# Three tiles move beside layer 0's buffers, and ScalarE writes the ones columns

## The chip, the core and the metric

The kernel runs on one core of one Trainium2 chip. The core has a matrix engine (TensorE, "PE" in the profile; its weight loads are "PEld"), a vector engine (VectorE, "DVE"), a scalar engine (ScalarE, "ACT"), a general engine (GpSimd, "POOL") and a sync engine (SyncE, "SP") that here only issues transfers. Each engine takes its instructions in a fixed order, and semaphores order the engines among each other. Transfers between device memory and the on-chip buffer (SBUF) are issued from SP ("SPq") or from ScalarE ("ACTq"). TensorE writes to PSUM, a second small memory, from which VectorE and ScalarE read. The metric is the time of one execution on the device in microseconds (us).

## The reference, cut to what matters

There are 16 graphs (batches) of 1024 nodes with 128 features each (`x`), and a symmetric 0/1 matrix `adj` per graph. Four layers follow one another, each as `x = layernorm(x + layer(x, adj))`:

```
layer 0:  w = row softmax of adj^T where adj^T != 0
          region = batchnorm((w @ x) @ K1 + b1);  people = batchnorm((w^T @ region) @ K2 + b2)
layer 1:  h = x W + b;  e = leaky_relu(h a1 + (h a2)^T + b_a) where adj > 0
          softmax over axis 1;  relu(attention @ h)
layers 2, 3:  scores = leaky_relu((h * a_k) @ h^T) where adj == k+1 (k = 0..3)
          softmax over the last axis;  alpha @ h
```

The two batch norms of layer 0 take their mean and variance over all 16 graphs and all nodes. So layer 0 has to pass over all graphs before its second norm is known, and only then can any graph go on to its residual, its layer norm and layers 1 to 3.

## The kernel before

`fast_path` (from L554) serves inputs whose matrix holds only zeros and ones; a check at its end calls `general_path` otherwise, and that isn't executed here.

**Layer 0 (L646 to L788).** Two pools of buffers, `f_l0` and `f_l0c`, are open. For each batch the kernel loads the matrix and its transpose (`load_adj`, L722, tiles `f_at` and `f_att` of 1 MB each, six buffers each) from SP, multiplies them on TensorE with three bf16 parts of the features (`product`, L733), sums the parts on VectorE (L736), and accumulates Gram matrices on TensorE (`gram`, L665). The result of each batch, `f_yf`, is written to a scratch array in device memory, `f_people`, from ScalarE's queue (L775).

**Between the layers (L790 to L835).** From the Gram matrix (copied out by ScalarE, L669) and a few sums a short chain computes the second batch norm: TensorE L800 to L808, VectorE L811 to L816, L602 and L603, then an inverse square root on GpSimd (`rsqrt`, L596 and L597), VectorE L606 to L609, three small products on TensorE (`on_rows`, L826). It ends in `f_m` (L829), the matrix that the batch's `people` values are to be multiplied with, and in two tiles of rows, `f_shift2_rows` (L831) and `f_row_rows` (L834).

**Layers 1 to 3 (from L840).** The pools of layer 0 are closed by then, and a pool `f_lanes` is opened over the same bytes. It holds three lanes (`Lane`, L843), so that three batches are under way at once, and tiles that all lanes share. A first access to a tile of that pool has to wait until everything that used the closed pools is done, the last write of `f_people` among it. The tiles that matter here are:

- `rows` (two per lane, L851): 1024 rows of 129 columns; the last column holds ones (written by GpSimd, L853), so that the products of layers 2 and 3 (L1206) give the sum of the weights along with the result;
- `xt` (one per lane, L854): turned rows, 128 x 1024;
- `nothing` (L872): zeros for an empty product (L1085);
- `yn` and `x0` (L876, one buffer each, shared by all batches): a batch's `people` values, read back from device memory (L1007), and its original features (L1009).

The profile leaves trailing numbers of tile names out: `x0` is `f_x` in its lines, `xt` is `f_xt`.

For each batch the steps after layer 0 begin with two loads (`yn`, then `x0`, on SP). VectorE adds the shift and the bias to `x0` (L1011, then eight times L1014). In three groups of rows TensorE turns `yn` (L980), ScalarE copies the turned rows to `xt` (L993), TensorE multiplies them with `f_m` (L1023), VectorE adds `x0` and writes `rows` (L1031). A layer norm follows (L906, L908, L918 to L924), the normed rows are turned in their turn (L980, L993), and layer 1 starts (L1056).

**Order.** All steps from there on are given to `Plan` (L107), which takes written starting times (`BEGIN`, `WHEN`) and costs, works out one order per engine, and ties each engine's instructions to that order. Layer 0 and the work between the layers aren't under it. They, and the plan's instructions among them, are put in order by the framework's own scheduler, which starts what is ready and prefers what stands earlier in the program. The profile shows such a move: VectorE executes L1238, from the very end of the program, at 395.04 us. The classes of shared tiles, their numbers and the plan's data stay as they are in this change.

## Time and profile before

| what | us |
|---|---|
| median of three runs | 1717.28 (1714.45 to 1718.93) |
| the profiled execution's own time | 1720.13 |
| its span, first to last instruction | 1718.2 |
| layer 0 and the work between the layers | from 0 to about 431 |
| last `f_people` write, issue (L775) | 423.57 |
| first load of `yn`, issue (L1007) | 427.24 |
| first load of `x0`, issue (L1009) | 427.64 |
| first product with `f_m` (L1023) | 432.38 |
| first product of layer 1 (L1056) | 446.81 |

The time outside the span is 1720.13 - 1718.2 = 1.9 us. TensorE is busy for 94% of the span, VectorE for 77%, ScalarE for 62%, GpSimd for 20%. The page's second part cuts the span into 40 slices of 43 us, and slice 10, from 430 us on, is the one in which TensorE is least busy (5 tenths, at 6 tenths of its clock): that is where layer 0 hands over to the lanes.

In a line of the timeline the first column is the start in us, the second the length in us (of the whole group where a line stands for several instructions, "xN"), then the engine, the line of the kernel, the operation and the tiles "out<-in". A bracket gives the idle time of the engine before it and what ended that.

### The profile page before, as it was taken

To read this page: it belongs to the slowest core of one execution; us is meant where nothing else is said; L and a number is where in the kernel's file an instruction comes from. 1 tells how busy PE (TensorE), PEld (TensorE's weight loads), DVE (VectorE), ACT (ScalarE), POOL (GpSimd) and SP (SyncE) were. 2 spreads that over 40 slices of the span, in tenths; PEclk is the share of its full clock that TensorE was granted. 3 is DMA by queue.
4 is the path that set the end of the run, shared out by engine and by line. 5 is a ranking of instruction groups with operands and counts; after the bars stand their busy time and mean duration, and the time that the engine had idled before them with its cause. 6 is when DMAs were issued, how large, how long until landed. Compare 5 with 4: busy or idle time off the path is not lost. (4 is left out here: it accounts for less than half of the span.)

```text
span 1718.2 us, 34517 instructions
## 1 busy us (share of the span) xinstructions
PE 1618.3 (94%) x13007; PEld 1450.2 (84%) x13023; DVE 1325.3 (77%) x2940; ACT 1070.8 (62%) x2697; POOL 339.3 (20%) x621
## 2 busy tenths in 40 slices
PE   6999999999569999999999999999999999999996
PEld 4666666666459999999999999999999999999995
DVE  4565575565558889898988989898898989888764
ACT  6555545642235767767676776767667676767664
POOL 0000000000222131323223232332314132231310
PEclk9999999999679999999999999999999999999998
DMA  8999999996355657677666767776676777666651
GB/s 306 381 370 390 361 377 381 368 384 224 132 167 173 200 172 219 196 208 212 208 196 187 219 194 212 209 210 191 190 216 195 205 215 211 189 180 202 183 161 52
DMA packets 394641, 397.14 MB, mean 231 GB/s; under 512 B 10592, under 2 KB 339168, under 8 KB 394464
## 3 DMA queue, kind: packets, MB, share of 16 engines
q1 hardware_dynamic: 377824, 386.45, 69.3%
q10 hardware_dynamic: 16640, 8.39, 1.6%
q8 instruction: 104, 1.70, 0.4%
q14 instruction: 73, 0.60, 0.1%
HBM read 377.89 MB, written 16.91 MB: 230 GB/s over the span
## 5 line engine op out<-in xcount | busy, mean ns | idle before, releaser
L1206 PE MATMUL f_pbank<-f_rows,f_p 128*128 128x129 f32 x4096 | 497.2, 274 | 1.7 <-ACT f_xt L993 1.0
L1206 PEld LDWEIGHTS f_pbank<-f_rows,f_p 128*128 128x128 f32 x4096 | 476.6, 191 | 2.9 <-ACT f_xt L993 1.4
L1156 PE MATMUL f_pbig<-f_xt,f_hw 128*128 128x128 f32 x2304 | 305.2, 277 | 3.5 <-ACT f_hw L995 2.5
L1156 PEld LDWEIGHTS f_pbig<-f_xt,f_hw 128*128 128x128 f32 x2304 | 282.5, 193 | 4.8 <-ACT f_hw L995 3.0
L1106 PE MATMUL f_pbig<-f_q,f_p 128*128 128x128 f32 x2048 | 258.8, 281 | 18.4 <-ACT f_q L1100 18.3
L1185 DVE TENSOR_TENSOR f_q<-f_q,f_e 128x1024 f32<-128x1024 f32 (+7 forms) x256 | 193.5, 756 | 103.7 <-ACT f_q L1178 67.0
L1178 ACT ACTIVATE f_q<-f_pbig,f_neg_shift 128x1024 f32<-128x1024 f32 (+7 forms) x256 | 189.0, 738 | 127.9 <-PE f_pbig L1170 123.2
L1106 PEld LDWEIGHTS f_pbig<-f_q,f_p 128*128 128x128 f32 x2048 | 246.7, 197 | 20.8 <-ACT f_q L1100 20.4
L1182 ACT ACTIVATE f_e<-f_pbig,f_neg_shift 128x1024 f32<-128x1024 f32 (+7 forms) x256 | 188.5, 736 | 58.5 <-PE f_pbig L1170 53.6
L1193 DVE TENSOR_TENSOR f_p<-f_q,f_a 128x1024 f32<-128x1024 f32 (+7 forms) x256 | 192.3, 751 | 2.1 <-issue 0.2
L733 PE MATMUL f_pz<-f_xs,f_at 128*128 128x390 bf16 x1024 | 180.5, 332 | 4.8 <-DVE f_xs L716 4.2
L733 PE MATMUL f_pz<-f_zs,f_att 128*128 128x390 bf16 x1024 | 181.0, 328 | 3.1 <-DVE f_yf L736 2.9
L754 ACT ACTIVATE f_junk<-f_at,f_sq_bias 128x1024 bf16<-128x1024 int32 x128 | 146.9, 1148 | 51.8 <-DVE f_yf L736 48.4
L1091 DVE SCALAR_TENSOR_TENSOR f_p<-f_u,f_r,f_u 128x1024 f32<-128x1024 f32 x128 | 162.8, 1272 | 2.1 <-DMA f_u<-f_u_dram 2.0
L733 PEld LDWEIGHTS <-f_at 128*128 128x128 fp8e4 x1024 | 100.6, 98 | 73.9 <-issue 7.8
L733 PEld LDWEIGHTS <-f_att 128*128 128x128 fp8e4 x1024 | 100.0, 98 | 69.6 <-issue 6.5
L1094 DVE SCALAR_TENSOR_TENSOR f_p<-f_p,f_a 128x1024 f32<-128x1024 f32 x128 | 155.8, 1217 | 0.8
L1197 DVE TENSOR_TENSOR f_p<-f_pbig,f_a 128x128 f32<-128x128 f32 (+6 forms) x224 | 152.1, 679 | 0.0
L736 DVE TENSOR_REDUCE f_zr<-f_pz 128x129 f32<-128x387 f32 x128 | 63.2, 551 | 113.3 <-PE f_pz L733 113.2
L1170 PE MATMUL f_pbig<-f_ident,f_q 128*128 128x128 f32 x896 | 135.5, 273 | 4.2 <-DVE f_q L1185 3.3
L968 POOL TENSOR_SCALAR f_ln_var<-f_sq 128x3 f32<-128x3 f32 (+2 forms) x96 | 35.6, 371 | 505.2 <-ACT f_junk L957 505.2
L993 ACT COPY f_xt<-f_pbank 128x512 f32<-128x512 f32 (+2 forms) x192 | 83.2, 441 | 71.8 <-PE f_pbank L980 71.7
(165 smaller groups left out, 2079.2 us busy)
## 6 DMA issues: line engine op xcount, KB each, us to landing
f_a<-in_adjt_dram SPq DMA_DIRECT2D x384, 512.0 KB, 4.7
f_at<-in_adj_dram SPq DMA_DIRECT2D x64, 1024.0 KB, 9.1
f_att<-in_adjt_dram SPq DMA_DIRECT2D x64, 1024.0 KB, 13.6
f_u<-f_u_dram SPq DMA_DIRECT2D x32, 512.0 KB, 6.2
f_xn<-in_x_dram SPq DMA_DIRECT2D x16, 512.0 KB, 11.2
f_people<-f_yf ACTq DMA_DIRECT2D x16, 512.0 KB, 16.9
f_yn<-f_people SPq DMA_DIRECT2D x16, 512.0 KB, 3.8
f_x<-in_x_dram SPq DMA_DIRECT2D x16, 512.0 KB, 6.6
```

Source lines behind the costliest of these rows:

```text
L733: nc.tensor.matmul(pz[:, :3 * K], a8[:, j % 2, c * 512:(c + 1) * 512:4], moving[:, j].rearrange("p k d -> p (k d)"), start=(j == 0), stop= ...
L754: nc.scalar.activation(junk, at[c // 2][:, c % 2, :], AF.Square, bias=sq_bias, accum_out=squares[:, b, c:c + 1])
L1091: p = op(DVE, 1.2, lambda e, t, t2, *_, j=j: nc.vector.scalar_tensor_tensor(e, t2, ln.r[:, j:j + 1], t, ALU.mult, ALU.max), [key("r", j)], ...
L1094: op(DVE, 1.24, lambda t, e, j=j: nc.vector.scalar_tensor_tensor(e, e, 1.0, t.rearrange("p c n -> p (c n)"), ALU.mult, ALU.mult, accum_out ...
L1106: nc.tensor.matmul(t[:, c * D:(c + 1) * D], q[:, c * P:(c + 1) * P], hn[:, j, :], start=False, stop=(j == C - 1 and c % 4 == 3))
L1156: nc.tensor.matmul(t[:, j * P:(j + 1) * P], hw[:, j * P:(j + 1) * P], xt[:, mine], start=True, stop=True)
L1178: nc.scalar.activation(q[:, blocks, :], t[:, c * P:].rearrange("p (c n) -> p c n", n=P), AF.Exp, bias=neg_shift)
L1182: nc.scalar.activation(e[:, c * P:], t[:, c * P:], AF.Exp, bias=neg_shift, scale=SLOPE)
L1185: nc.vector.tensor_max(q[:, blocks, :], q[:, blocks, :], e[:, c * P:].rearrange("p (c n) -> p c n", n=P))
L1193: nc.vector.tensor_mul(t[:, c * P:].rearrange("p (c n) -> p c n", n=P), q[:, blocks, :], k[:, c:, :])
L1197: nc.vector.tensor_mul(t[:, :c * P].rearrange("p (c n) -> p c n", n=P), s[:, :c * P].rearrange("p (c n) -> p c n", n=P), k[:, :c, :])
L1206: nc.tensor.matmul(t[:, :D + 1], w[:, j * P:(j + 1) * P], xl[:, j, :], start=(j == 0), stop=(j == C - 1))
```

## The change

Four edits, all in `fast_path`:

1. `nothing` and its zeroing by GpSimd move from after the lanes to the constants at the start of the function.
2. Three tiles, `yn`, `x0` and `xt0` (4 KB per partition each), are taken from the pool of constants, which is open all along, so their bytes aren't shared with layer 0's buffers. `yn` and `x0` are the shared tiles of before under the same names; `xt0` becomes the `xt` of lane 0. The other two lanes keep theirs in the pool of lanes. All later tiles move by 13 KB per partition.
3. The six columns of ones are written by ScalarE, as a copy of eight columns of a tile of ones, in place of six GpSimd memsets.
4. The classes `yn` and `x0` of the plan are given the new tiles.

```diff
 LANES = 3
+EARLY = ("yn", "x0", "xt0")
...
+    nothing = const.tile([P, 512], BF16, name="f_nothing")
+    nc.gpsimd.memset(nothing, 0.0)
+
+    early = {name: const.tile([P, C, D], F32, name=f"f_{name}") for name in EARLY}
+
     sums = const.tile([P, 3, B * C], F32, name="f_sums")
...
             for t in self.rows:
-                nc.gpsimd.memset(t[:, :, D:D + 1], 1.0)
-            self.xt = tile([P, N], "xt")
+                nc.scalar.copy(t[:, :, D], ones[:, :C])
+            self.xt = early["xt0"].rearrange("p c n -> p (c n)") if i == 0 else tile([P, N], "xt")
...
-    nothing = lanes.tile([P, 512], BF16, name="f_nothing")
-    nc.gpsimd.memset(nothing, 0.0)
...
-    for cls, n in (("yn", 1), ("x0", 1)):
-        plan.tiles(cls, [lanes.tile([P, C, D], F32, name=f"f_{cls}{i}") for i in range(n)])
+    for cls in ("yn", "x0"):
+        plan.tiles(cls, [early[cls]])
```

## The prediction

> **What bounds the kernel now.** I read the page's first two parts, then busy times by stretch, then the timeline and the waits around 430 us, where layer 0 hands over to the lanes.

> ```profile
> span 1718.2 us, 34517 instructions
> PE   6999999999569999999999999999999999999996
> PEclk9999999999679999999999999999999999999998
> DMA  8999999996355657677666767776676777666651
> ```

> TensorE bounds both long stages, at 9 tenths or more in nearly every slice. The dip in slices 10 and 11 is the handover, where the time goes by a chain of waits and not by any engine's work. Busy time by stretch (start and end, length, then busy us of PE, PEld, DVE, ACT and POOL with instruction counts, the granted clock, DMA share, GB/s):

> ```profile
> 423.50:427.20 3.70, 2.73 (x23) 2.44 (x22) 1.55 (x9) 0.27 (x1) 0.19 (x1) 0.97 0.49 142
> 427.20:450.80 23.60, 14.32 (x54) 11.49 (x54) 9.91 (x41) 7.16 (x20) 5.65 (x21) 0.50 0.29 90
> 450.80:515.00 64.20, 35.92 (x206) 32.56 (x209) 39.06 (x93) 19.96 (x67) 18.12 (x24) 0.77 0.50 169
> ```

> From 427.20 to 450.80 no engine is busy for more than 14.32 of 23.60 us, and the clock is at half. The change acts there. Its timeline:

> ```profile
> 407.09 0.88 SPq L722 DMA_DIRECT2D f_att<-in_adjt_dram  x2
> ...
> 423.57 0.52 ACTq L775 DMA_DIRECT2D f_people<-f_yf  x1
> ...
> 427.24 0.34 SPq L1007 DMA_DIRECT2D f_yn<-f_people  x1
> 427.35 0.29 POOL L853 MEMSET f_rows<- 128x8 f32 x6 [3.55 <-DMA f_people<-f_yf]
> 427.46 0.16 DVE L603 TENSOR_TENSOR f_bn_var<-f_got,f_bn_var 128x1 f32<-128x1 f32 x1
> 427.56 0.52 POOL L873 MEMSET f_nothing<- 128x512 bf16 x1
> 427.64 0.43 SPq L1009 DMA_DIRECT2D f_x<-in_x_dram  x1
> 428.05 0.19 POOL L596 TENSOR_SCALAR f_rs_t<-f_bn_var 128x1 f32<-128x1 f32 x1
> ...
> 430.31 0.29 DVE L829 TENSOR_TENSOR f_m<-f_m,f_pacc 128x128 f32<-128x128 f32 x1 [0.42 <-PE f_pacc L826]
> 430.79 0.27 ACT L831 COPY f_shift_rows<-f_pacc 128x128 f32<-128x128 f32 x1 [5.76 <-PE f_pacc L826]
> ...
> 430.92 0.85 PE L980 MATMUL f_pbank<-f_ident,f_yn 128*128 128x128 f32 x3
> ...
> 431.85 0.48 ACT L993 COPY f_xt<-f_pbank 128x384 f32<-128x384 f32 x1 [0.42 <-PE f_pbank L980]
> ...
> 432.38 1.65 PE L1023 MATMUL f_pbank<-f_m,f_xt 128*128 128x128 f32 x6 [0.61 <-ACT f_xt L993]
> 433.01 1.23 DVE L1011 TENSOR_TENSOR f_x<-f_x,f_shift_rows 128x1024 f32<-128x1024 f32 x1 [2.41 <-DMA f_x<-in_x_dram]
> ...
> 437.74 0.69 DVE L1031 TENSOR_TENSOR f_rows<-f_pbank,f_x 128x512 f32<-128x512 f32 x1 [0.74 <-PE f_pbank L1023]
> ```

> See three things. The `yn` load, the first memset and everything else that touches the lanes' pool start at about 427.2, when the last `f_people` write has landed. GpSimd's inverse square root, on the path to `f_m`, starts when the memsets end, though its input was there at 427.46 + 0.16 = 427.62. And between `f_m` (430.31 + 0.29 = 430.60) and the first product with it (432.38) stand the turns of `yn` and the copy to `xt`, while VectorE waits for `x0` until 433.01.

> **The change part by part**

> *The two loads.* Outside the shared bytes, `x0` waits for nothing and `yn` for batch 0's write of `f_people`, issued at 56.0. SP takes instructions in order; the scheduler prefers what stands earlier in the program, and all layer 0 loads do. I therefore place both behind the last `f_att` issue, at 407.09 + 0.88 = 408.0. SP has nothing to do then until 427.24, so nothing is queued behind them that is late; the third load of the plan, the second `yn`, still waits for L980. Landing now takes about 3.8 us for a `yn` and 5.2 us for this `x0`; behind the `f_att` loads and beside the 408.70 `f_people` write (whose kind takes 3.5 to 17.8 us) I bound it by 17.8: on chip by 426, before anybody asks. Cost there: nothing, covered by 15 us in which TensorE multiplies tiles whose loads are ahead in the same queue. At worst the 1 MB delays that `f_people` write, which nobody waits for.

> [...]

> *The inverse square root.* Six memsets (0.29 us together) and `f_nothing` (0.52) leave GpSimd's queue there. The hop from L603 to L596 in the first norm was 0.1 us (415.02 to 415.11), so L596 starts at 427.71 instead of 428.05: 0.34 us gained for `f_m`, `f_shift2_rows` and `f_row_rows`. The zeroing of `nothing` at the start costs GpSimd 0.52 us beside loads whose first product comes at 14.8: nothing.

> *The ones on ScalarE.* Six copies of 128x8. The nearest rows are L1064 (170 ns for 128x3) and L1075 (255 ns for 16x128): 1.0 to 1.5 us. They wait for the landing at 427.2 and so end by 428.8. ScalarE is idle from 425.03 to 430.79 (the 5.76 us in L831's bracket), now to 430.45: hidden, with 1.6 us to spare. Behind them stand L993 or L831; if that cover were gone they would cost at most 1.5 us.

> *The turned rows.* `xt0` is free and `yn` is there, so the first group's turns need only a PSUM bank, which layer 0 gives up with ScalarE's copy L669 (424.76 + 0.27 = 425.03). TensorE is idle from about 426.6 to 429.5. Three turns (0.85 us at half clock, less at full) and the copy (0.48) fit in there. Should the turns stand ahead of L808 they delay the norm by up to 0.3 us (three at the full-clock pace of 0.11 us); I take 0. The plan's order lets only this one group go ahead: the second group's turns stand behind the first product with `f_m`.

> *The sum on the path.* TensorE's `on_rows` products end their issue 0.34 earlier; the last of six starts at 430.70 and one follows each 0.21 us, so L1023 starts at 430.70 - 0.34 + 0.21 = 430.57, `f_m` being ready at 430.26. It started at 432.38: 1.81 us gained. L1011 starts behind L831, at 430.79 + 0.27 - 0.34 + 0.08 = 430.80 and not at 433.01: 2.2 us gained, so `x0` isn't late any more. Next late is TensorE: L1031 of the second group waited 0.74 us for L1023 already, and its turns and products follow L1023 at an unchanged pace. The gain is the smaller, 1.81 us. Everything behind (the norm, layer 1's start at 446.81, the second `yn` load at 437.88, the loads of `u`) follows by waits on this chain, in an unchanged order, so I carry 1.8 us to the end.

> Against the profiled execution: 1720.1 - 1.8 = 1718.3 us. That execution stands 2.85 us over the median of the runs (1717.28), so the time is 1717.3 - 1.8 = 1715.5, with 1.5 (turns ahead of L808) and 2.2 (TensorE gains with `x0`) as its ends.

> **The rivals**

> *The clock comes back earlier.* It is at half for 23.9 us from 427.0 on and changes several more times until 515.7, always at ends of stretches of about 3.4 us. Work between 427.2 and 450.8 keeps TensorE busy for 14.32 us; one more such stretch at full clock saves at most 1.7 us, and in the ramp to 515 (clock 0.77) a second one as much. For it: the chain's products stand closer together. Against it: the idle gaps behind 436 stay. Time: 1717.3 - 1.8 - 1.7 to 3.4 = 1712.1 to 1713.8, take 1713. A row can't tell where the 3.4 us stretches will lie in another run; the same slip can cost 1.7.

> [...]

> *The loads are not freed.* If the scratch array counts as one whole, `yn` still waits for the last `f_people` write and lands at 430.7, `x0` behind it at 432.9. Then only the 0.34 us remain: 1717.0. Against it: nothing in the layer 0 rows ties one batch's write to the next's.

> *The loads stand among layer 0's (the other side).* If the scheduler puts `yn` in an earlier gap of SP, SP stands still there until the `f_people` write has landed, 16.9 us in the median, while layer 0 is short of room: DMA is at 9 tenths or more, and TensorE has no wait on loads there. Once the block and 1 MB more (2.8 us at the 370 GB/s of those slices) exceed the lead of the loads over the products, TensorE stops. Price between 0 and 16.9 + 2.8 = 19.7; the nearest row is SP's present wait on `f_people`, 15.4 us per batch, which TensorE survives without a wait, so most is covered: I take 5 us. Time: 1717.3 - 1.8 + 5 = 1720.5. It decides from a stop of 1.8 us on. Against it: full queues leave SP no gap in which a later load would be preferred.

> *The ones stand ahead of L669 on ScalarE.* L669 (424.76) would then wait for 427.2 and six copies: 427.2 + 1.5 - 424.8 = 3.9 us later, and all behind it: 1719.4. Against it: GpSimd's memsets are executed behind later work of layer 0, and L669 is ready first.

> **How the numbers follow.** Chances: 1.8 us gained 0.58, clock 0.15, loads not freed 0.09, loads among layer 0's 0.10, ones ahead of L669 0.04, the moved addresses or anything else 0.04. The predicted time is the first's, 1715.5. The runs of before spread over 4.5 us, 0.3% of 1717; less than 0.3% (5.2 us) can hardly be told from no change, so the bounds are 1712.1 and 1722.4. The range from 1711.0 to 1720.0 holds the first case with half that spread (2.2 us to either side: 1713.3 to 1717.7), most of the clock's, the unfreed loads and the ones, and a lighter form of the slower rival. Faster by over 0.3% is the clock's case with its better end and the first case on a good run: 0.32. Slower is the loads among layer 0's in its heavier form: 0.10. Within: 0.58.

> **What would show it.** Right: issues of `yn` and `x0` at about 408, L980's first three turns and one L993 before 429, L596 within 0.1 us of L603, L1023 at L829's end, L1011 behind L831, and layer 1 starting at 445.0. Wrong: a `yn` issue before 407 with TensorE waits on `f_at`, L596 or L669 late behind copies, a first L1011 that still waits for a load, or half-clock time before 515 that differs by more than 3.4 us from 54.6.

## The result

Over 22 runs each, beside one another, the changed kernel takes 1714.70 us in the median (1710.87 to 1718.98) and the kernel before 1717.75 (1712.78 to 1722.02). The ratio of the times is 0.9979, with a 95% interval from 0.9972 to 0.9986: 3.6 us less, between 2.4 and 4.8 (the medians differ by 3.05). The prediction had 1.8 us less.

The profiled execution of the changed kernel has a span of 1713.2 us (before: 1718.2). From its page, the first line, then the slices of TensorE and of its clock:

```profile
span 1713.2 us, 34530 instructions
PE   6999999999469999999999999999999999999996
PEclk9999999999789999999999999999999999999998
```

The dip in slices 10 and 11 is still there, but the clock in them is at 7 and 8 tenths instead of 6 and 7. The same three stretches as before show it better (start and end, length, busy us of PE, PEld, DVE, ACT and POOL with counts, granted clock, DMA share, GB/s):

```profile
423.50:427.20 3.70, 3.00 (x26) 2.72 (x25) 1.27 (x7) 0.64 (x2) 0.20 (x1) 1.00 0.49 142
427.20:450.80 23.60, 13.27 (x63) 10.52 (x64) 10.73 (x44) 8.94 (x33) 4.96 (x14) 0.71 0.13 46
450.80:515.00 64.20, 37.32 (x238) 34.23 (x237) 38.94 (x93) 21.77 (x65) 16.91 (x24) 0.81 0.54 180
```

From 427.20 to 450.80 the clock is 0.71 instead of 0.50. The timeline of the handover; line numbers are four to six higher than before (L1011 and L1013 load `yn` and `x0`, L602 is the inverse square root, L984 turns, L1027 multiplies with `f_m`, L1015 adds to `x0`, L1035 writes `rows`):

```profile
408.01 0.46 SPq L1011 DMA_DIRECT2D f_yn<-f_people  x1
408.52 0.60 SPq L1013 DMA_DIRECT2D f_x<-in_x_dram  x1
...
426.21 0.52 PE L984 MATMUL f_pbank<-f_ident,f_yn 128*128 128x128 f32 x3
426.57 0.28 PE L814 MATMUL f_pacc<-f_ones,f_mm 128*128 128x1 f32 x2
...
427.20 0.86 ACT L859 COPY f_rows<-f_ones 128x8 f32<-128x8 f32 x6
...
427.98 0.19 POOL L602 TENSOR_SCALAR f_rs_t<-f_bn_var 128x1 f32<-128x1 f32 x1 [4.20 <-DVE f_bn_var L609]
...
429.93 0.29 DVE L835 TENSOR_TENSOR f_m<-f_m,f_pacc 128x128 f32<-128x128 f32 x1
...
430.49 1.49 PE L1027 MATMUL f_pbank<-f_m,f_xt 128*128 128x128 f32 x6
430.60 1.22 DVE L1015 TENSOR_TENSOR f_x<-f_x,f_shift_rows 128x1024 f32<-128x1024 f32 x1 [0.39 <-ACT f_shift_rows L837]
...
433.51 1.16 PE L1027 MATMUL f_pbank<-f_m,f_xt 128*128 128x128 f32 x8 [0.68 <-ACT f_xt L997]
...
434.77 0.69 DVE L1035 TENSOR_TENSOR f_rows<-f_pbank,f_x 128x512 f32<-128x512 f32 x1 [0.19 <-PE f_pbank L1027]
```

Both loads are issued at 408, the turns of the first group are done before the norm is, and the first product with `f_m` starts at 430.49 instead of 432.38: 1.89 us earlier. Then the gain grows, which it wasn't to do. The second group's addition to `rows` (the last line) starts at 434.77 instead of 437.74, 2.97 us earlier, because the products ahead of it take 1.16 us and not the 2.08 they took at half clock.

VectorE executes its 2940 instructions in the same order in all kernels here, so I can subtract start times one by one. This shift against the kernel before is -0.01 us at 422, where layer 0 ends; counted from there it is -2.96 at 440, -3.02 at 511, and -5.63 from 520 on, where it stays until 1400; at the end of the span it is -4.98. So in this pair of executions there are two jumps to the better, one by 440 and one of 2.6 us between 511 and 520, and near the end a part is lost again. The second lies where layer 2 of the first lane starts. In the kernel before, one stretch there and VectorE's wait behind it:

```profile
512.14:515.56 3.42, 3.42 (x18) 3.42 (x18) 0.97 (x4) 1.49 (x5) 0.00 (x0) 0.50 1.16 306
```
```profile
520.25 1.23 DVE L1185 TENSOR_TENSOR f_q<-f_q,f_e 128x1024 f32<-128x1024 f32 x1 [7.14 <-ACT f_q L1178]
```

And in the changed kernel, where the same work lies some 3 us earlier:

```profile
508.50:511.91 3.41, 2.74 (x23) 2.50 (x23) 1.55 (x5) 1.73 (x5) 0.00 (x0) 0.99 1.11 314
```
```profile
514.61 1.23 DVE L1189 TENSOR_TENSOR f_q<-f_q,f_e 128x1024 f32<-128x1024 f32 x1 [4.52 <-ACT f_q L1182]
```

Before, TensorE is busy all through that stretch at clock 0.50, and VectorE waits 7.14 us; after, the clock is 0.99 and the wait is 4.52. The theory to test was therefore: a direct part of about 1.9 us, as forecast, and a part that is clock. The rivals: all direct, or not the tiles at all but the ones columns.

### The profile page after: what moved, and what is told of

Same layout as the page of the kernel before. It is cut to its first block, busy times and chain, and to the rows that moved or that the text cites. A ratio compares the mean times of both kernels' runs of the same rounds, so it can differ in the third digit from the quotient of the medians.

```text
span 1713.2 us, 34530 instructions
## 1 busy us (share of the span) xinstructions
PE 1615.4 (94%) x13023; PEld 1447.6 (84%) x13023; DVE 1325.4 (77%) x2940; ACT 1071.7 (63%) x2703; POOL 338.3 (20%) x615
```

## The experiments

**The tiles alone.** The ones and the zero tile stay with GpSimd, behind the release of layer 0's buffers.

```
-                nc.scalar.copy(t[:, :, D], ones[:, :C])
+                nc.gpsimd.memset(t[:, :, D:D + 1], 1.0)
... (the zero tile back behind the lanes)
```

> The three early tiles alone; the ones columns and the zero tile stay with GpSimd behind the release of layer 0's buffers. Theory (the tiles carry it: the first product with f_m comes about 1.9 us earlier because the two loads no longer wait for a landing at 430.7 and 432.9, and the clock that comes back earlier adds 1 to 3 us): 2.7 to 3.8 us below the kernel before, as much as the whole change; the first inverse square root at 428.0, and f_m a few hundredths to 0.3 us later than with the whole change. Rival (the ones columns, by clearing GpSimd's queue, carry a good part): no more than 1.8 us below the kernel before.

Measured: ratio 0.9976 (0.9964 to 0.9987), as the whole change. The three tiles carry all of it that the ratios can show.

**The ones alone**, with the zero tile early and no tile moved.

> The ones columns by ScalarE and the zero tile early, no tile moved. Theory (tiles carry it): GpSimd's inverse square root starts near 427.7 instead of 428.05 as nothing is ahead of it, f_m is ready 0.3 us earlier, but the first y still lands at 430.7 and the first x at 432.9, so the first product with f_m stays within 0.3 us of 432.4: 0 to 0.3 us below the kernel before. Rival (ones carry it): 1.5 us or more below.

Measured: 0.9997 (0.9988 to 1.0006). The inverse square root came 0.35 us earlier (0.34 forecast), and nothing followed from it: the first turns wait for `yn` as before.

**x's tile back in the lanes; y's tile back in the lanes.**

```
-    for cls in ("yn", "x0"):
-        plan.tiles(cls, [early[cls]])
+    plan.tiles("yn", [early["yn"]])
+    plan.tiles("x0", [lanes.tile([P, C, D], F32, name="f_x0")])
```

> The changed kernel with x's tile back among the lanes' (y and the first turned rows stay early). Theory (both loads were late, and x's addition is as much on the path as the product with f_m): x's load is issued at about 427.3 and, as the only load at that time, lands between 430.5 and 432; its first addition starts there instead of at 430.6, and the first addition to rows starts behind it at 434.8 to 436: 1.5 to 3.3 us below the kernel before, so up to 2 us of the change's gain is lost. Rival (only y's load was late): no difference from the changed kernel.

> The changed kernel with y's tile back among the lanes' (x and the first turned rows stay early). Theory (both loads were late, y's by as much as the turns, their copy and the first product take behind it): y's load is issued near 427.2, as the only load at that time, and lands at 430.4 to 431; the first product with f_m at 431.8 to 432.5 instead of 430.49, the second behind it at 435 or so instead of 433.51, and the first additions to rows 1 to 2 us later than in the changed kernel: the shift at 440 us is 1 to 2 us instead of 3.0, and the whole 1.5 to 3 us below the kernel before. Rival (x's chain of nine additions alone sets the first rows): no difference from the changed kernel.

Measured: x back, 0.9978 (0.9968 to 0.9989); y back, 1.0006 (0.9994 to 1.0017). With x back, its first addition waits for the load and comes 1.1 us later than in the changed kernel (counted from layer 0's end); of the shift at 440 us 0.8 is lost (2.14 instead of 2.96), too little to show in the ratio. With y back the whole gain is lost, more than I had expected, and the trace says why: SP issues x's load at 427.31, behind y's at 426.92, and both are late.

```profile
426.92 0.34 SPq L1011 DMA_DIRECT2D f_yn<-f_people  x1
427.31 0.43 SPq L1013 DMA_DIRECT2D f_x<-in_x_dram  x1
```

So the second run undid both loads and doesn't weigh y against x.

**The turned rows back in lane 0's own tile.**

> The changed kernel with lane 0's turned rows back in the lane's own tile (y and x stay early). The copy of the first three turned chunks then waits for the write of the last rows (landing near 427.2) instead of running at 426.83, and the first product with f_m waits for f_m until 430.49 anyway. Theory (that place is worth nothing): first product with f_m and all behind it within 0.1 us of the changed kernel, 3 to 3.7 us below the kernel before. Rival (ScalarE's copies crowd into the time in which the scale and shift are spread over the rows): the first addition to x 0.3 to 0.6 us later.

Measured: 0.9983 (0.9972 to 0.9994). The first product with `f_m` starts 0.36 us later than in the changed kernel; 0.32 of that is `f_m` itself, made by products that ran at half clock in this execution. In total it can't be told from the changed kernel.

**The norm's product ahead of the turns.** In the changed kernel the early turns (426.21) stand ahead of the norm's last product (426.57 instead of 426.22). Here the plan's first TensorE instruction is tied behind it.

```
     nc.tensor.matmul(ps[:, 2:3], mm, ones[:, 0:1], start=True, stop=True)
+    norm_product = nc.cur_bb.bb.instructions[-1]
...
-        queued = {}
+        queued = {ins.engine: ins.name for ins in behind}
...
-    plan.run()
+    plan.run((norm_product,))
```

> The changed kernel, with TensorE's planned work told to start behind the norm's last product, so that the three early turns can't stand ahead of it. Theory (the turns took 0.35 us of the path that ends at f_m): the norm's last product at 426.2 instead of 426.57, the inverse square root near 427.7 instead of 427.98, the first product with f_m and the first addition to x 0.25 to 0.35 us earlier than in the changed kernel, so 0.3 us below it in all (3.4 to 4 us below the kernel before), if no stretch of half clock moves with it. Rival (f_m isn't what the first rows wait for, or the clock's windows take it back): no difference from the changed kernel within 0.15 us.

Measured: 0.9977 (0.9965 to 0.9988), no difference from the changed kernel. The inverse square root did come 0.28 us earlier. But this execution's first stretch of half clock began at 427.1 (430.0 in the changed kernel; layer 0 ended 1.5 us earlier here), the three small products behind the norm took 1.65 us instead of 1.29, and the first product with `f_m` started no earlier. The 0.3 us are there and are smaller than what the clock does to the same instructions.

**Loads among layer 0's**, the slower rival of the prediction.

```
             yf = spread(b - 1, *held) if b else None
+            if b == 1:
+                nc.sync.dma_start(early["yn"], people[0].rearrange("p (c d) -> p c d", d=D))
+                nc.sync.dma_start(early["x0"], x[0].rearrange("(c p) d -> p c d", p=P))
... (batch 0's loads in the plan left out)
```

> The changed kernel with batch 0's loads of y and x issued within layer 0, right behind the first batch's rows are written, so that they stand ahead of later batches' loads of edges in SP's queue. It prices the slower way that the prediction kept. Theory of the prediction (each wait of SP behind the write of the rows puts off the edges of a layer that TensorE and the loads bound): layer 0 ends 2 to 5 us later, so that the whole is between the kernel before and 2 us above it. Rival (layer 0 has enough edges loaded ahead, six tiles of each kind): as the changed kernel, 3 to 3.7 us below the kernel before.

Measured: 1.0017 (1.0007 to 1.0026), 2.9 us slower than before, where at most 2 was expected. SP's waits between 20 and 90 us have this line (waiting line, what it waited for, us, times, longest):

```profile
SPq L794 <- DMA f_people<-f_yf: 13.8, 1, 13.8
```

and behind it TensorE stops, because a tile of the matrix isn't there yet:

```profile
66.28 4.84 PE L739 MATMUL f_pz<-f_xs,f_at 128*128 128x390 bf16 x28 [3.25 <-DMA f_at<-in_adj_dram]
```

The shift is 3.7 us at 63 us, and 3.86 at 422: one stop that layer 0 never makes good. The rival was real and its price of 5 us near. The changed kernel avoids it only because the framework's order puts the loads at 408 us.

**TensorE kept at work, layer 1's turns.** TensorE idles for 5.09 us ahead of the first turns of normed rows. Products of zeros (128x512, bf16), which change no result, fill that; they go into the bank that the turns overwrite.

```
+                for _ in range(zeros if g == 0 else 0):
+                    nc.tensor.matmul(pt, nothing[:, :P], nothing, start=True, stop=True)
                 for k, c in enumerate(group(g)):
                     nc.tensor.transpose(pt[:, k * P:(k + 1) * P], src(c, *rest), ident)
```

> The changed kernel with twenty products of zeros (128x512, bf16, the form that takes 0.22 to 0.3 us each in layer 1's start) ahead of the first turns of normalized rows of batch 0, where TensorE idles for 5.09 us from 436.1 to 441.2; the zeros go into the bank that the turns then overwrite. Theory (a stretch in which TensorE idles is followed by a stretch at half clock, and part of the gain was such a stretch): the granted clock from 440 to 447 is 1 instead of 0.5, the eight turns and sixteen products of the first lane at 441.2 to 447.6 take half as long, layer 1's first step starts 2 to 3 us earlier, and the whole is 2 to 3.5 us below the changed kernel (5 to 7 below the kernel before). Rival (the clock there is hidden behind the loads of edges and of the two rows of factors, and the gain was all direct): within 0.5 us of the changed kernel.

Measured: 0.9999 (0.9990 to 1.0008), no gain. My edit caught the same helper's turns in layer 3 as well, where TensorE is full:

```profile
548.20 4.48 PE L984 MATMUL f_pbank<-f_nothing 128*128 128x512 bf16 x20
```

The shift, 1.2 to 1.7 us better than the changed kernel's from 451 to 511, fell by 3.8 us there. Without that second set:

> The changed kernel with the twenty products of zeros only ahead of layer 1's first turns of batch 0; the run before this one put twenty more ahead of batch 0's turns in layer 3, where TensorE has no idle time, and 3.8 us were lost there between 552 and 562 us. Theory (idle TensorE is what brings the half clock, and the half clock is on the path): the shift against the kernel before is some 4.2 to 4.8 us at 450 to 511 us (the changed kernel: 3.0 to 3.15), because the turns and products at 440 to 447 run at full clock; behind that it is larger by 2.6 to 3.3 us where the last stretch of half clock is 6.8 us long, and by nothing where it is 10.2. In all 1 to 1.5 us below the changed kernel in the median, 4.3 to 5 us below the kernel before. Rival (the loss at 552 was not the zeros' but the plan's answer to an earlier start): again no faster than the kernel before.

Measured: 0.9968 (0.9956 to 0.9980), 1712.59 us against 1718.39. The shift at 451 us, counted from 422, is 4.35 instead of the changed kernel's 3.15, as the theory has it; at 511 only 3.46 against 3.02 is left, with half clock in this execution from 454.7 to 475.2 us. The interval overlaps the changed kernel's, so the ratios alone don't separate the two.

**TensorE kept at work in every gap to layer 2.** First with the places guessed, then with the places read from the first one's trace (ahead of layer 1's step products with `start=False`, so that zero is added to their sums; both also have the norm's product ahead of the turns).

```
             def product(q, t, j=j):
+                for _ in range((34, 8, 8, 0, 12, 0, 0, 0)[j] if b == 0 else 0):
+                    nc.tensor.matmul(t[:, :512], nothing[:, :P], nothing, start=False, stop=False)
```

> The changed kernel with the norm's last product ahead of the early turns, and products of zeros wherever TensorE idles for more than 2 us between 426 and 505 us in batch 0: nine behind the norm's last product, twenty ahead of layer 1's turns, 34, 15, 17 and 6 ahead of the products of layer 1's steps 0, 2, 5 and 7 (adding zero to their sums), sixteen and nine ahead of the first two groups of turns of layer 2. Theory (the granted clock of a stretch of 3.4 us follows from TensorE's work in the one before, and three quarters of the 4 us that the kernel can win here are clock): half clock between 426 and 516 us falls from 37.5 us in the changed kernel to less than 14, VectorE's wait before its first layer 2 product (7.14 us before, 4.52 after) falls to about 4.5 or less in every execution, and the whole ends 3 to 5.5 us below the changed kernel, 6.5 to 9 below the kernel before. Rival (the zeros stand in the way of the real products, or the loads of edges end the waits anyway): within 1 us of the changed kernel.

> The kernel that filled all gaps, with its products of zeros put where the trace of that run had the idle time: 34, 8, 8 and 12 ahead of the products of layer 1's steps 0, 1, 2 and 4 (before: 34, 15, 17 and 6 ahead of steps 0, 2, 5 and 7), and in layer 2 fourteen ahead of the group that is turned first and six ahead of the next (before: sixteen and nine ahead of groups that were not first, so that 6.46 and 2.11 us of zeros ran after 503.7 us with real work behind them). Theory (the zeros cost nothing while TensorE idles, their own length where it doesn't, and save the half clock that would follow): no half clock of more than 7 us in all between 426 and 516 us, a shift against the kernel before of 5 to 6 us at 511 and 7.5 to 9 us behind 520 (less the offset of the two traces at 422), and in all 2 to 4 us below the version with zeros ahead of layer 1's turns alone, 7 to 9 us below the kernel before. Rival (the last stretch of half clock comes from elsewhere, or some zeros stand in the way again): no faster than that version, 4 to 6 us below the kernel before.

Measured: 1.0017 (1.0007 to 1.0027) for the guess, 0.9959 (0.9946 to 0.9971) with the places read. The guess had sixteen zeros in front of layer 2's real work:

```profile
503.71 6.46 PE L988 MATMUL f_pbank<-f_nothing 128*128 128x512 bf16 x16
```

It brought half clock between 426 and 520 down to 13.7 us and was still slower than before: full clock was worth nothing here, bought with the time of a busy engine. In the second the zeros run where nothing else does, half clock is 6.8 us there, and VectorE's wait is down to 3.36 us:

```profile
509.43 1.23 DVE L1198 TENSOR_TENSOR f_q<-f_q,f_e 128x1024 f32<-128x1024 f32 x1 [3.36 <-ACT f_q L1191]
```

It takes 1709.44 us in the median (1707.93 to 1711.54) against 1718.07. Its interval lies below the changed kernel's, so it beats both kernels.

**The kernel before, kept at work in the same way.** With the clock the same, what is the change worth?

> The kernel before (three tiles among the lanes', ones columns by GpSimd) with the zero tile early and the same products of zeros as in the version that filled the gaps at their own places, and six more ahead of batch 0's first turns, so that TensorE stays at full clock in both. It asks what the change is worth when the clock is the same with and without it. Theory (the change is worth a direct 1.8 to 2.4 us, and the rest of its measured 3.6 us was half clock that came out differently): half clock between 426 and 516 us no more than 10 us; the first product with f_m near 432.2; 1.5 to 2.6 us slower than the version with the change and the same zeros, so 6 to 7.2 us below the kernel before. Rival (the change's gain was all clock): as fast as the version with the change, 8.5 us below the kernel before. Rival (the gain was all direct): 3.3 us or more slower than that version, no more than 5.3 us below the kernel before.

Measured: 0.9964 (0.9952 to 0.9976), 1711.42 us against 1716.73: without any tile moved, zeros alone take off 6.2 us (4.1 to 8.2). The interval overlaps that of the version with the change and the same zeros, so the ratios don't separate the two kernels, and they don't rule out the rival that the gain was all direct, which had at most 5.3 us here. The traces say more. From 426 to 450.8 us both run at full clock (the version with the change first, then this one):

```profile
426.00:450.80 24.80, 17.89 (x103) 11.54 (x105) 10.92 (x45) 9.62 (x34) 4.94 (x14) 1.00 0.19 61
```
```profile
426.00:450.80 24.80, 17.97 (x102) 11.13 (x100) 10.78 (x45) 8.34 (x27) 5.23 (x20) 1.00 0.29 89
```

There the shift differs by 2.1 us at 440, 2.0 at 451 and 2.25 at 511. That is the direct worth of the change with the clock the same: full up to 451, and 6.8 us of half clock in each from there to 511. What sets it is `x0` (with the change, then without):

```profile
430.51 1.23 DVE L1022 TENSOR_TENSOR f_x<-f_x,f_shift_rows 128x1024 f32<-128x1024 f32 x1 [0.39 <-ACT f_shift_rows L841]
431.09 0.94 PE L1034 MATMUL f_pbank<-f_m,f_xt 128*128 128x128 f32 x6 [0.63 <-ACT f_xt L1004]
433.95 1.15 DVE L1042 TENSOR_TENSOR f_rows<-f_pbank,f_x 128x384 f32<-128x384 f32 x2
```
```profile
431.44 0.94 PE L1030 MATMUL f_pbank<-f_m,f_xt 128*128 128x128 f32 x6 [0.61 <-ACT f_xt L1000]
431.72 1.23 DVE L1018 TENSOR_TENSOR f_x<-f_x,f_shift_rows 128x1024 f32<-128x1024 f32 x1 [2.53 <-DMA f_x<-in_x_dram]
435.16 1.15 DVE L1038 TENSOR_TENSOR f_rows<-f_pbank,f_x 128x384 f32<-128x384 f32 x2
```

Layer 0 ends 0.94 us later in the first of the two. Counted from there, the addition to `x0` starts 2.15 us earlier with the change, because it doesn't wait for its load, and so does the first write of `rows`, which stands right behind the eight additions that follow. The first product with `f_m` starts only 1.29 us earlier, since a turn of `yn` stands behind the small products in that version (430.18). At full clock no row waits for it.

At 530 the profiled pair is 6.2 apart, because this kernel still met one stretch of half clock at the start of layer 2 (506.5 to 509.9), and waited 7.34 us behind it.

**All the profiled executions together.** The shift of VectorE's instructions against the kernel before, counted from layer 0's end (422 us), and when the last half clock of that time ended, in times of the kernel before (the end minus the whole shift at 511, not only the part since 422):

| kernel | shift at 451 | at 511 | at 530 | half clock 426 to 520, us | last half clock ended |
|---|---|---|---|---|---|
| before | 0 | 0 | 0 | 54.6 | 515.7 |
| changed | -3.15 | -3.02 | -5.63 | 37.5 | 511.6 |
| tiles alone | -2.67 | -2.50 | -5.82 | 51.2 | 510.8 |
| ones alone | -0.15 | -1.66 | -0.91 | 51.2 | 515.7 |
| norm first | -3.72 | -3.91 | -7.10 | 34.1 | 511.0 |
| turned rows back | -1.46 | -1.13 | -1.38 | 47.8 | 515.2 |
| x back | -1.98 | -1.52 | -0.79 | 47.8 | 515.7 |
| y back | +0.75 | -0.42 | -0.50 | 58.0 | 515.5 |
| loads in layer 0 | -3.28 | -4.04 | -4.16 | 44.4 | 515.5 |
| zeros at two places | -4.33 | -4.68 | -4.02 | 30.7 | 515.5 |
| zeros, layer 1's turns | -4.35 | -3.46 | -6.73 | 34.1 | 510.8 |
| gaps filled | -4.63 | -6.88 | -10.66 | 6.8 | 504.3 |
| before, gaps filled | -2.63 | -4.63 | -4.42 | 10.2 | 515.6 |

(The guessed places are left out, since zeros stood in the way there.) Between 511 and 530 each row either gains 2.6 to 3.8 us, and then half clock had ended by 511.6, or changes by less than 0.8 us either way, and then it ended after 515. Nothing lies between. So the second jump is one stretch of 3.4 us more or less at half clock over the start of layer 2. It doesn't go by the edits alone: the kernel with the turned rows back keeps both early loads and lacks it, and the one with zeros at two places holds the whole change and lacks it too. The pair of executions that the result was first read from shows the change on its lucky side.

Something like it comes once more near the end. Between 1650 and 1695 us the shift changes by less than 0.1 us in the six profiles with 3.4 us of half clock there, as in the kernel before. In the one with none (zeros, layer 1's turns) it gets 1.6 us better, and in the six with 6.8 us or more it gets 1.05 to 2.64 us worse. The changed kernel is one of those: its lead is 5.8 us at 1650 and 4.7 us at 1695.

## Why the prediction was right or wrong

*What bounds it, the loads, the ones.* Right. The loads were issued at 408.01 and 408.52 (408.0 forecast), layer 0 was unmoved (shift -0.01 us at 422), and the ones ran from 427.20 for 0.86 us beside other work. `yn` landed after 9.5 us and `x0` after 11.5, within the bound of 17.8. The last two `f_att` loads, ahead of them in the same queue, landed after 5.07 and 7.32 us (4.88 and 7.90 before), and the `f_people` write on ScalarE's queue after 11.02 (9.18 before).

*The turns.* I took 0 for turns ahead of the norm's last product, with up to 0.3 as the other end. It was 0.35. So L602 came 0.07 us earlier and not 0.34. That this cost nothing in the sum was luck: half clock began at 430.0 in this execution and at 427.0 before, and the three small products behind the norm took 1.29 us instead of 1.65.

*The sum.* L1023 was to start at 430.57 and L1011 at 430.80; they started at 430.49 and 430.60. The direct gain of 1.81 us was near: 1.89 in the pair, 2.0 to 2.25 with the clock the same. But it was taken as the smaller of two gains, that of the first product with `f_m`. With the clock the same it was the other one that reached the rows, that of the addition to `x0` (2.2 forecast, 2.15 measured). That the two lay so close was luck.

*"At an unchanged pace ... so I carry 1.8 us to the end."* This is the step that failed, and by a size: the clock's term, put at 0. Layer 1's products started at 444.00 and not at the forecast 445.0, and the sign I had named, half-clock time before 515 that differs by more than 3.4 us from 54.6, came with 37.5. Each run has its mean granted clock on record. With the rest of the span at full clock, a mean of 0.9819 over 89 runs of the kernel before is 2 x 0.0181 x 1716 = 62 us of the span at half, and 0.9836 over 22 runs of the changed one is 56 us. Among those 22 runs the span grows by 0.29 us per us of half clock (r = 0.69); 5.8 us less of it are then 1.7 us, and 2.0 + 1.7 = 3.7 us, near the 3.6 measured. In the kernel before the same slope is 0.09 (r = 0.33), which would give 0.5, so this split is an estimate; that the clock takes part is what the zeros showed.

*The rivals.* The clock's (0.15, 1713) was half of the truth: it came on top of the direct gain, on average with no more than the lower end of the 1.7 to 3.4 us that I gave it. I had argued against it with the gaps behind 436, which stay; but a gap need not close for the stretch before it to count. Loads not freed, and ones ahead of L669: neither happened. Loads among layer 0's: it didn't happen, and when made to, SP waited 13.8 us (15.4 to 16.9 in the prediction's rows) and layer 0 lost 3.86 us (5 taken).

*"Can hardly be told from no change."* The prediction said that of any difference under 0.3%. With 22 runs of each kernel, the gain of 0.21% has an interval from 0.14% to 0.28%, which leaves no change out.

## What to carry to other kernels

Where a chain of waits hands one stage over to the next, a gain on the chain also moves the work against the clock's stretches (3.4 us more or less at half clock went with 2.6 to 3.8 us here); put a term for it in the range, and compare several executions before a jump in one pair is read as the change's. Tiles whose loads could go early shouldn't share bytes with a stage that ends late, and a load issued earlier must not stand in a queue ahead of loads that are needed sooner (layer 0 lost 3.86 us here). Work that only keeps TensorE busy paid where the trace showed it idle (0.9959 with the gaps to layer 2 filled); where it wasn't, 4.48 us of zeros cost 3.8 us here.

## What the runs showed of the hardware

```profile
433.41:436.83 3.42, 1.93 (x11) 1.41 (x11) 3.23 (x14) 0.31 (x2) 0.20 (x2) 0.99 0.18 48
436.83:440.24 3.41, 0.00 (x0) 0.00 (x0) 1.39 (x9) 0.93 (x3) 2.86 (x8) 0.51 0.69 262
```

TensorE was busy for 1.93 us of the first, and the second was at 0.51. With products of zeros the clock was 1.00 from 426.00 to 450.80; without them it was 0.71 from 427.20 on in the changed kernel. The stretches don't lie at the same place of the work in every execution: the first half clock began at 430.05 in the changed kernel, and at 427.42 with the turned rows back, where layer 0 ends 1.30 us earlier. After the same work that is 1.3 us apart, and not a whole stretch. So the same instruction stands at another place in the stretches in these two executions. At the start of layer 2 one stretch of half clock more or less went with 2.6 to 3.8 us between one profile and another; how much of the spread of one kernel's runs it makes isn't shown.
